# The last image's depthwise stage laid out over four engines by a list scheduler inside the kernel

## The chip, the cores and the metric

The kernel runs on one NeuronCore of a Trainium2 chip. The metric is device time in microseconds, the median of three runs. Five instruction streams work side by side[...]: TensorE (PE in the profile, its weight loads PEld), VectorE (DVE), ScalarE (ACT), GpSimd (POOL) and SyncE (SP), which here issues transfers.

## The reference, cut to what matters

Four residual layers run over four images of 256 channels and 64x64 pixels, all in float32. The change touches layer 2, whose weights are made from the image itself:

```python
def _L2_conv_ref(x, Wd1, bd1, Wd2, bd2, Wp1, bp1, Wp2, bp2, bias):
    dk = _gen_kernel(x, Wd1, bd1, Wd2, bd2).reshape(B, C, K, K)   # 3x3 taps for each image and channel
    pk = _gen_kernel(x, Wp1, bp1, Wp2, bp2).reshape(B, O, C)      # 256x256 matrix for each image
    dw = lax.conv_general_dilated(xr, kr, (STRIDE, STRIDE), [(PAD, PAD), (PAD, PAD)],
                                  feature_group_count=B * C)      # 3x3 depthwise, K = 3
    out = jnp.einsum('bchw,boc->bohw', dw, pk) + bias[None, :, None, None]
    return out
...
    x = x + _L2_conv_ref(_gn(x), ...)   # layer 2
    x = x + _L3_conv_ref(_gn(x), ...)   # layer 3: needs the group statistics of all of layer 2
```

`_gen_kernel` takes the mean over all pixels of a small hidden layer and multiplies it out, so no tap is known before the whole normalised image is.

## The kernel before

Channels are two halves `h` of 128 partitions. Pixels are four parts of 1024 (16 rows) or eight blocks of 512 (8 rows), one block to a PSUM bank. There are eight banks, handed out by `bank`[...]. `xp` holds the normalised image with a row of zeros above and below; `big` holds the residual, which for the last image lies in `tpg[:, 0:2]`.

Instructions are recorded by Python generators, and the order of recording is the order on each engine (`tc.manual_schedule`). For images 0 to 2 the layers of one image are woven into the attention of the next. The last image has nothing left to be woven into, so from about 2,800 us on its layers run alone, and the engines have to be filled by hand. One filler exists: layer 3 of image 2 is held back as 16 pieces (`held`). `w.fill(n)` issues the two matmuls of n pieces; `w.settle()` issues ScalarE's addition of the bias (L1819) and the store (L1820) for what was filled. A second filler is `warm(n)` (L355), 2n small matmuls on constants whose result nobody reads.

The last image's layer 2 is `generated` with `diag` set. Its steps:

- Group statistics (`group_finish`), then `hidden` (PE L1526, ACT L1529), whose sums over the pixels give `pooled`; a matmul spreads it over the partitions (L1550), and four small VectorE instructions make `dk`, the 2 x 9 taps of each partition.
- `shared_out` computes the depthwise outputs `dw`. Part i is (c, h): parts 0, 2, 4, 6 are half 0, parts 1, 3, 5, 7 half 1. `centre` (ACT L1572) writes the middle tap and `taps` (DVE, all through the helper `stt`, L140) adds the other eight, `dw = xp * dk + dw`, in SBUF. Parts 3 and 5, and seven taps of part 1, are done by TensorE instead: `taps_by_products` multiplies `xp` with a diagonal matrix of each tap (ACT L1674 makes the nine, PE L1631 multiplies) and ScalarE copies the bank out (L1634).
- `mix_kernel` makes `pk` by eight VectorE instructions from the four slices `wp2`, loaded at L1517.
- For each block of 512 pixels and each half of the outputs two matmuls with `pk` (L1580, and L1723 for the last part), then VectorE adds the result to the residual and sums it (L1592), and ScalarE squares and sums that (L1597).
- The sums and sums of squares of all 16 such pieces are needed (L385) before `mixed`, the last image's layer 3, can begin.

The order between these is written by hand in `shared_out`, for instance

```python
            dw[2] = centre(2)
            diagonal(27)
            go(0, 8)
            w.settle()
            mix_kernel(slices, range(0, R // 2))
            go(2, 3)
```

where `go(i, n)` takes n taps of part i on VectorE and `diagonal(n)` n products on TensorE. GpSimd does nothing in this stage.

## Time and profile before

| what | us |
|---|---|
| median of 3 runs (lowest, highest) | 2986.73 (2986.69, 2986.93) |
| the profiled execution's own time | 2988.41 |
| its span, from first to last instruction | 2986.7 |
| busy in the span: TensorE, VectorE, ScalarE, GpSimd | 2934.1, 1798.8, 1328.7, 136.8 |
| the last image's `dk` ready | 2862.28 |
| last residual sum of layer 2 ends (VectorE) | 2937.0 |
| last square ends, statistics begin | 2938.69 |
| first matmul of the last image's layer 3 | 2949.36 |

The span is 1.7 us shorter than that execution's time, and the execution 1.7 us longer than the median. Starts and durations below are microseconds from the span's start. A row of the timeline is one instruction or a merged run of like ones: start, time, engine, source line, operation, output<-inputs, shapes, count. [...]each matmul of the program is two records.

### The profile page before, as it was taken

To read this page: it belongs to the slowest core of one execution; us is meant where nothing else is said; L and a number is where in the kernel's file an instruction comes from. 1 tells how busy PE (TensorE), PEld (TensorE's weight loads), DVE (VectorE), ACT (ScalarE), POOL (GpSimd) and SP (SyncE) were. 2 spreads that over 40 slices of the span, in tenths; PEclk is the share of its full clock that TensorE was granted. 3 is DMA by queue.
4 is the path that set the end of the run, shared out by engine and by line. 5 is a ranking of instruction groups with operands and counts; after the bars stand their busy time and mean duration, and the time that the engine had idled before them with its cause. 6 is when DMAs were issued, how large, how long until landed. Compare 5 with 4: busy or idle time off the path is not lost.

```text
span 2986.7 us, 31274 instructions
## 1 busy us (share of the span) xinstructions
PE 2934.1 (98%) x11678; PEld 1785.7 (60%) x11678; DVE 1798.8 (60%) x2785; ACT 1328.7 (44%) x2674; POOL 136.8 (5%) x185
## 2 busy tenths in 40 slices
PE   7999999999999999999999999999999999999998
PEld 3454555566566666777576666777647544456744
DVE  8737667751645854675455583667154568854584
ACT  2234333445656344225665543323656554433732
POOL 0000000001011000000011000000100100000100
PEclk9999999999999999999999999999999999999999
DMA  6245544224323012111620303111440223443021
GB/s 227 74 85 122 67 67 75 39 32 99 113 39 43 22 78 75 57 57 33 188 37 11 50 8 124 57 54 49 92 92 11 25 42 46 32 95 90 24 69 68
DMA packets 371295, 199.38 MB, mean 67 GB/s; under 512 B 305664, under 2 KB 315648, under 8 KB 367616
## 3 DMA queue, kind: packets, MB, share of 16 engines
q1 hardware_dynamic: 71328, 175.81, 17.5%
q10 hardware_dynamic: 295200, 4.72, 7.9%
q0 software_dynamic: 4608, 16.78, 3.7%
q8 instruction: 94, 1.54, 0.2%
q14 instruction: 65, 0.53, 0.1%
HBM read 131.18 MB, written 82.87 MB: 72 GB/s over the span
## 4 chain that ended last, share of the span: by engine, by line
PE 76%; issue 19%; DVE 2%; ACT 2%; POOL 0%; DMA 0%; ACTq 0%; DVEq 0%; POOLq 0%
PE pf L1013 24%; PE py L1129 16%; PE py L1126 8%; PE ps_tp L951 4%; PE ps_ex L1811 4%; PE ps_qk L1316 3%; PE ps_pw L1580 3%; PE ps_conv L663 2%; PE ps_ctx L1343 2%; PE ps_o L1414 2%; PE ps_g L956 2%; PE ps_dw L1631 1%; PE ps_wy L1066 1%; ACT big L760 1%; PE ps_xt L1296 1%
## 5 line engine op out<-in xcount | busy, mean ns | idle before, releaser
L1014 ACT ACTIVATE pr<-pf 128x512 f32<-128x512 f32 x1024 | 602.7, 596 | 911.3 <-PE pf L1013 889.9
L1013 PE MATMUL pf<-tpg 128*128 128x512 f32 x2048 | 966.4, 594 | 0.0
L1013 PEld LDWEIGHTS pf<-tpg 128*128 128x128 f32 x2048 | 374.1, 190 | 358.4 <-issue 336.4
L1129 PE MATMUL py<-pr,tpg 128*128 128x512 f32 x1152 | 541.6, 592 | 0.9 <-ACT pr L1014 0.9
L1126 PEld LDWEIGHTS py<-tpg,pr 128*128 128x128 f32 x3584 | 434.9, 192 | 108.0 <-issue 100.7
L1126 PE MATMUL py<-tpg,pr 128*128 128x129 f32 x3584 | 436.3, 275 | 2.4 <-ACT pr L1014 2.4
L1129 PEld LDWEIGHTS py<-pr,tpg 128*128 128x128 f32 x1152 | 218.6, 190 | 277.4 <-issue 268.3
L137 DVE TENSOR_TENSOR tot<-tot,pr 128x1024 f32<-128x1024 f32 x252 | 307.6, 1221 | 98.5 <-ACT pr L1014 98.0
L140 DVE SCALAR_TENSOR_TENSOR dw<-xp,dk,dw 128x1008 f32<-128x1008 f32 x208 | 263.3, 1270 | 8.0 <-ACT dw L1572 2.4
L663 PE MATMUL ps_conv<-v,u 128*128 128x256 f32 x864 | 195.6, 379 | 2.3 <-DVE v L137 2.3
L663 PEld LDWEIGHTS ps_conv<-v,u 128*128 128x128 f32 x864 | 161.5, 190 | 31.3 <-issue 8.4
L951 PE MATMUL ps_tp<-big,wtpg_s 128*128 128x512 f32 x256 | 117.1, 596 | 4.7 <-ACT big L760 4.0
L232 POOL TENSOR_TENSOR rstd<-rstd,half 128x2 f32<-128x2 f32 x24 | 17.5, 731 | 2173.4 <-DVE rstd L427 2063.0
L137 DVE TENSOR_TENSOR tpg<-ps_g,bg_s 128x512 f32<-128x512 f32 x32 | 22.1, 692 | 155.2 <-PE ps_g L956 155.2
L1316 PE MATMUL ps_qk<-wqkv_s,xg 128*128 128x256 f32 x496 | 113.6, 379 | 0.0
L140 DVE SCALAR_TENSOR_TENSOR sums<-ps_conv,sums 128x512 f32<-128x512 f32 x72 | 49.8, 691 | 103.9 <-PE ps_conv L663 97.5
L1316 PEld LDWEIGHTS ps_qk<-wqkv_s,xg 128*128 128x128 f32 x496 | 93.8, 190 | 20.4 <-issue 8.4
L1580 PE MATMUL ps_pw<-dw,pk 128*128 128x512 f32 x216 | 97.4, 592 | 0.0
L951 PEld LDWEIGHTS ps_tp<-big,wtpg_s 128*128 128x128 f32 x256 | 45.8, 190 | 54.7 <-issue 41.8
L952 ACT ACTIVATE tpg<-ps_tp,btp_s 128x512 f32<-128x512 f32 x64 | 44.0, 687 | 70.4 <-PE ps_tp L951 70.4
L1079 DVE COPY total<-py 128x2 f32<-128x2 f32 x28 | 4.5, 159 | 115.6 <-PE py L1126 115.6
L1819 ACT ACTIVATE res<-ps_ex,b 128x512 f32<-128x512 f32 x56 | 38.1, 688 | 76.5 <-PE ps_ex L1811 74.6
(400 smaller groups left out, 3280.3 us busy)
## 6 DMA issues: line engine op xcount, KB each, us to landing
u<-filters SPq DMA_DIRECT2D x72, 256.0 KB, 2.6
xp<-in_x_dram SPq DMA_DIRECT2D x16, 1024.0 KB, 8.4
xs_d<-big POOLq DMA_DIRECT2D x32, 512.0 KB, 6.3
wy_d<-wt SPq DMA_DIRECT2D x32, 512.0 KB, 2.8
wy<-wy_d SPq DMA_DIRECT2D x32, 512.0 KB, 4.7
out_dram<-res SPq DMA_DIRECT2D x64, 256.0 KB, 2.0
xs_d<-in_x_dram SPq DMA_DIRECT2D x24, 512.0 KB, 6.6
xs<-xs_d SPq DMA_DIRECT2D x24, 512.0 KB, 5.2
```

Source lines behind the costliest of these rows:

```text
L137: nc.vector.tensor_tensor(o, a, b, op)
L140: nc.vector.scalar_tensor_tensor(o, a, s, b, op0, op1)
L663: nc.tensor.matmul(ps[:, bass.ts(oh, IY * IX)], u[i][:, h, bass.ts(oh, P)], v[:, i, bass.ts(h, IY * IX)], start=(h == 0), stop=(h == NH - 1))
L951: nc.tensor.matmul(ps, wtpg_s[:, h, k, :], big[:, h, cols], start=(h == 0), stop=(h == NH - 1))
L956: nc.tensor.matmul(ps[:, j, :], big[:, h, bass.ts(4 * c + j, P)], wtpg_s[:, h, 2, :], start=(h == 0), stop=(h == NH - 1))
L1013: nc.tensor.matmul(pf, phi[:, bass.ts(2 * m + s, P)], theta[:, bass.ts(q, 512)], start=True, stop=True)
L1014: nc.scalar.activation(pr[:, bass.ts(s, 512)], pf, AF.Exp)
L1126: nc.tensor.matmul(py[t // 2][:, t % 2, :], probs[i][:, s * 512 + t * P:s * 512 + (t + 1) * P], g[:, 2 * m + s, :], start=(begin and t % 2 ...
L1129: nc.tensor.matmul(py, g[:, 2 * m + s, 0:P], probs[i][:, bass.ts(s, 512)], start=begin, stop=end)
L1316: nc.tensor.matmul(ps[:, 0:2 * HID], xg[:, h, bass.ts(j, P)], wqkv_s[:, h, 0:2 * HID], start=(h == 0), stop=(h == NH - 1))
L1580: nc.tensor.matmul(ps, pk[:, h * NH * P + oh * P:h * NH * P + (oh + 1) * P], dw[h][:, bass.ts(s, 512)], start=(h == 0), stop=(h == NH - 1))
L1811: nc.tensor.matmul(ps, wm[h][:, bass.ts(oh, P)], big[:, h, bass.ts(c, 512)], start=(h == 0), stop=(h == NH - 1))
```

## The change

The hand-written order of `shared_out` goes, with `taps_by_products`. In its place `halves_of_three` splits the work into 16 half parts `(k, h)`, a block of 512 pixels of one half of the channels, and gives each to one engine: five to GpSimd (`ON_POOL`), three wholly to TensorE and two in part (`ON_TENSOR` counts the products), the rest to VectorE. VectorE's taps now accumulate in a PSUM bank; only the last one writes SBUF. GpSimd's part is the addition alone: ScalarE first writes the scaled tap into one of five SBUF tiles of 512 (the free end of `tpg[:, 2]`), and GpSimd adds it. `mix_kernel` becomes `mixing`, which accumulates in a bank too. All of it, the squares and the additions left over from `fill` included, is a list of jobs with an engine, a duration, predecessors and a rank; `emit_by_start` places them by these durations, and the order of the result is the order of recording. The durations serve for nothing else.

Around it five calls change: `fill(2)` becomes `fill(3)` at the end of linear attention, `warm(3)` becomes `fill(1)` after the statistics of layer 2, `settle` and `fill(1)` between the `hidden` blocks go, `fill(3)` after the pooling matmul becomes `fill(1)`, and 16 small matmuls of `warm` ahead of layer 3's statistics become `fill(1)`. The loads of `wp2` are issued behind that of `pk`, before the normalisation.

```diff
-            w.fill(2)
+            w.fill(3)
...
+    ENDING = [t for t in TAPS if t[1] != 1] + [(0, 1), (2, 1)]
+    ALL = [(1, 1)] + ENDING
+    ON_POOL = ((0, 0), (1, 1), (2, 0), (4, 1), (6, 0))
+    ON_TENSOR = {(0, 1): 1, (3, 1): 7, (5, 1): 9, (6, 1): 9, (7, 1): 9}
+    HALVES = [(0, 0), (3, 0), (1, 0), (3, 1), (7, 0), (5, 0), (0, 1), (6, 0), (6, 1), (2, 1), (2, 0), (4, 0), (1, 1), (5, 1),
+              (7, 1), (4, 1)]
+    TAP_TILES = 5
...
+    def emit_by_start(jobs, free, banks):
...
+                    if on == engine and all(a in ends for a in after) and len(spare) >= takes:
+                        at = [ends[a][1] + (0.2 if ends[a][0] != on else 0.0) for a in after]
+                        ready.append((max([free[on]] + at + sorted(spare)[:takes]), rank, j))
...
         if diag is not None:
-            warm(3)
+            w.fill(1)
...
+        if diag is not None:
+            slices = [load_wp2(j) for j in range(R // 2)]
...
-            if c == NC3:
+            if c == NC3 and diag is None:
                 w.settle()
                 w.fill(1)
...
-        w.fill(3)
+        w.fill(3 if diag is None else 1)
...
+            def middle(k, h, bank_of):
+                if bank_of:
+                    banks[k, h] = bank("ps_acc")
+                nc.scalar.activation(pixels(banks[k, h] if bank_of else half_tile(k, h)), xin[:, h, bass.ts(k, RB), :],
+                                     AF.Copy, scale=weight(h, (1, 1)))
...
+                    to = half_tile(k, h) if t == ENDING[-1] else acc
+                    stt(pixels(to)[:, :, x0:x1], src, weight(h, t), pixels(acc)[:, :, x0:x1], ALU.mult, ALU.add)
...
+                nc.scalar.activation(pixels(scaled_taps[n])[:, :, x0:x1], src, AF.Copy, scale=weight(h, t))
...
+                nc.gpsimd.tensor_tensor(acc, acc, pixels(scaled_taps[n])[:, :, x0:x1], ALU.add)
...
+            for n, f in enumerate(w.unsettled):
+                job(("late", n), E.Activation, 0.66, [], 4 + 1.5 * n, f, 0, ["late"])
...
+            emit_by_start(jobs, {E.PE: 0.5, E.Activation: 0.1, E.DVE: 0.0, E.Pool: 0.0}, 8 - late)
...
-        mv, gm, rstd = yield from group_finish(st, avg8, 1e-5, sh, (), (8, 1) if alone else (0, 0))
+        if alone:
+            w.fill(1)
+        mv, gm, rstd = yield from group_finish(st, avg8, 1e-5, sh, (), (0, 1) if alone else (0, 0))
```

On each engine the recorded order after `dk` begins as follows. VectorE: eight of `mixing`, four taps of (0,1), eight of (3,0), eight of (1,0). ScalarE: middle and taps of (0,0) with the nine diagonals between them. TensorE: one product of (0,1), nine of (6,1), seven of (3,1). GpSimd: the eight additions of (0,0), (6,0), (2,0), (1,1) and (4,1) in turn. The last on TensorE, VectorE and ScalarE are the matmuls, sums and squares of block 4.

More of the change, by code (lines that the diff above doesn't have):

```diff
@@ L1486, in conv_preact_fast @@
     TAPS = [(i, j) for i in range(3) for j in range(3) if (i, j) != (1, 1)]
+    ENDING = [t for t in TAPS if t[1] != 1] + [(0, 1), (2, 1)]
[6 more added lines that the diff above has]
+    def emit_by_start(jobs, free, banks):
+        ends, spare, left = {}, [0.0] * banks, list(jobs)
+        while left:
+            best = None
+            for engine in free:
+                ready = []
+                for j in left:
+                    name, on, us, after, rank, emit, takes, frees = j
+                    if on == engine and all(a in ends for a in after) and len(spare) >= takes:
+                        at = [ends[a][1] + (0.2 if ends[a][0] != on else 0.0) for a in after]
+                        ready.append((max([free[on]] + at + sorted(spare)[:takes]), rank, j))
+                if ready:
+                    first = min(r[0] for r in ready)
+                    pick = min((r for r in ready if r[0] <= first + 0.05), key=lambda r: r[1])
+                    if best is None or pick[0] < best[0]:
+                        best = pick
+            start, _, (name, on, us, after, rank, emit, takes, frees) = best
+            left.remove(best[2])
+            emit()
+            free[on] = start + us
+            ends[name] = on, free[on]
+            spare = sorted(spare)[takes:] + [free[on] + 0.1] * len(frees)
     def generated(w, b, big, k4, st, sh, diag):
+        if diag is not None:
+            diag, diag_all = diag
         if diag is None:
@@ L1518, in load_wp2 @@
             return t
+        if diag is not None:
+            slices = [load_wp2(j) for j in range(R // 2)]
         def hidden(g):
@@ L1565, in generated @@
         rows = CH // HW
+        if diag is not None:
+            diag_rest = diag_all[:, 9 * P:]
         PARTS = [(c, h) for c in range(N // CH) for h in range(NH)]
@@ L1616, in taps @@
                 yield 0.66
-        def taps_by_products(parts):
-            for i, some in parts:
-                c, h = PARTS[i]
-                dw[i] = k4("dw")
-                for s in range(2):
-                    ps = bank("ps_dw")
-                    dst = ps.rearrange("p (y x) -> p y x", x=HW)
-                    for n, (ty, tx) in enumerate([(1, 1)] + some):
-                        dx = tx - 1
-                        x0, x1 = max(0, -dx), min(HW, HW - dx)
-                        y0 = (2 * c + s) * RB + ty
-                        nc.tensor.matmul(dst[:, :, x0:x1], diag[:, 3 * ty + tx, :], xp[:, h, y0:y0 + RB, x0 + dx:x1 + dx],
-                                         start=(n == 0), stop=(n == len(some)))
-                        if n == len(some):
-                            nc.scalar.copy(dw[i][:, bass.ts(s, 512)], ps)
-                        yield
         def mix_kernel(slices, js):
@@ L1665, in in_order, with halves_of_three @@
             yield from w.pending()
-        def shared_out():
-            slices = [load_wp2(j) for j in range(R // 2)]
+        def halves_of_three():
             yield from w.pending()
-            products = taps_by_products([(1, TAPS[:6]), (3, TAPS), (5, TAPS)])
-            dw[0] = centre(0)
-            for k in range(9):
-                nc.scalar.activation(diag[:, k, :], ident, AF.Copy, scale=dk[:, 9 + k:10 + k])
-            on_vector = {i: taps(i) for i in (0, 2, 4, 6)}
-            on_vector[1] = taps(1, TAPS[6:])
-            def go(i, n):
-                for _ in range(n):
-                    next(on_vector[i])
-            def diagonal(n):
-                for _ in range(n):
-                    next(products)
-            def point(c):
-                d = [dw[2 * c + h] for h in range(NH)]
-                return [(2 * c + s, pointwise_products(s, d)) for s in range(2)]
-            dw[2] = centre(2)
-            diagonal(27)
-            go(0, 8)
-            w.settle()
-            mix_kernel(slices, range(0, R // 2))
-            go(2, 3)
-            mix_kernel(slices, range(R // 2, R))
-            go(1, 2)
-            go(2, 5)
-            dw[4] = centre(4)
-            res = point(0)
-            diagonal(5)
-            pointwise_added(*res[0])
-            go(4, 1)
-            pointwise_added(*res[1])
-            go(4, 7)
-            dw[6], dw[7] = centre(6), centre(7)
-            res = point(1)
-            diagonal(18)
-            go(6, 1)
-            pointwise_added(*res[0])
-            go(6, 2)
-            pointwise_added(*res[1])
-            go(6, 5)
-            ends = [taps(7, TAPS, slice(s * RB, (s + 1) * RB)) for s in range(2)]
-            for _ in ends[0]:
-                pass
-            res = point(2)
-            banks = [[bank("ps_pw") for _ in range(NH)] for _ in range(2)]
-            def half(s, h):
-                for oh in range(NH):
-                    nc.tensor.matmul(banks[s][oh], pk[:, h * NH * P + oh * P:h * NH * P + (oh + 1) * P],
-                                     dw[6 + h][:, bass.ts(s, 512)], start=(h == 0), stop=(h == NH - 1))
-            half(0, 0)
-            half(0, 1)
-            half(1, 0)
-            pointwise_added(*res[0])
-            for _ in ends[1]:
-                pass
-            half(1, 1)
-            pointwise_added(*res[1])
-            for s in range(2):
-                pointwise_added(6 + s, banks[s])
@@ new lines, in halves_of_three, with job, pixels, half_tile @@
+            scaled_taps = [diag_rest[:, bass.ts(n, 512)] for n in range(TAP_TILES)]
+            tiles, banks, wide = {}, {}, 63 / 64
+            jobs, chain = [], []
+            def job(name, engine, us, after, rank, emit, takes=0, frees=()):
+                jobs.append((name, engine, us, after, rank, emit, takes, frees))
+            def pixels(t):
+                return t.rearrange("p (y x) -> p y x", x=HW)
+            def half_tile(k, h):
+                if (k // 2, h) not in tiles:
+                    tiles[k // 2, h] = k4("dw")
+                return tiles[k // 2, h][:, bass.ts(k % 2, 512)]
@@ new lines, in shifted, with weight @@
+            def shifted(k, h, ty, dx):
+                x0, x1 = max(0, -dx), min(HW, HW - dx)
+                return x0, x1, xp[:, h, k * RB + ty:(k + 1) * RB + ty, x0 + dx:x1 + dx]
+            def weight(h, t):
+                return dk[:, h * 9 + 3 * t[0] + t[1]:h * 9 + 3 * t[0] + t[1] + 1]
+            def middle(k, h, bank_of):
[3 more added lines that the diff above has]
+                                     AF.Copy, scale=weight(h, (1, 1)))
@@ new lines, in on_vector, with scaled_tap @@
+            def on_vector(k, h, some):
+                acc = banks[k, h]
+                for t in some:
+                    x0, x1, src = shifted(k, h, t[0], t[1] - 1)
+                    to = half_tile(k, h) if t == ENDING[-1] else acc
+                    stt(pixels(to)[:, :, x0:x1], src, weight(h, t), pixels(acc)[:, :, x0:x1], ALU.mult, ALU.add)
+                if to is not acc:
+                    del banks[k, h]
+            def scaled_tap(k, h, t, n):
+                x0, x1, src = shifted(k, h, t[0], t[1] - 1)
+                nc.scalar.activation(pixels(scaled_taps[n])[:, :, x0:x1], src, AF.Copy, scale=weight(h, t))
@@ new lines, in on_pool, with on_tensor @@
+            def on_pool(k, h, t, n):
+                x0, x1, _ = shifted(k, h, t[0], t[1] - 1)
+                acc = pixels(half_tile(k, h))[:, :, x0:x1]
+                nc.gpsimd.tensor_tensor(acc, acc, pixels(scaled_taps[n])[:, :, x0:x1], ALU.add)
+            def on_tensor(k, h, some, last):
+                if some[0] == ALL[0]:
+                    banks[k, h] = bank("ps_dw")
+                for t in some:
+                    x0, x1, src = shifted(k, h, t[0], t[1] - 1)
+                    nc.tensor.matmul(pixels(banks[k, h])[:, :, x0:x1], diag[:, 3 * t[0] + t[1], :], src,
+                                     start=(t == ALL[0]), stop=(t == last))
@@ new lines, in taken, with diagonals, mixing @@
+            def taken(k, h):
+                nc.scalar.copy(half_tile(k, h), banks.pop((k, h)))
+            def diagonals(some):
+                for ty, tx in some:
+                    nc.scalar.activation(diag[:, 3 * ty + tx, :], ident, AF.Copy, scale=weight(1, (ty, tx)))
+            def mixing(j):
+                first, last = j == 0, j == R - 1
+                if first:
+                    banks["pk"] = bank("ps_pk")
+                acc = banks["pk"]
+                stt(pk if last else acc, slices[j // 2][:, j % 2, :], pb[:, R + j:R + j + 1], pk if first else acc,
+                    ALU.mult, ALU.add)
+                if last:
+                    del banks["pk"]
@@ new lines, in point, with added @@
+            def point(k, oh):
+                ps = banks[k, "out", oh] = bank("ps_pw")
+                for h in range(NH):
+                    nc.tensor.matmul(ps, pk[:, h * NH * P + oh * P:h * NH * P + (oh + 1) * P],
+                                     tiles[k // 2, h][:, bass.ts(k % 2, 512)], start=(h == 0), stop=(h == NH - 1))
+            def added(k, oh):
+                cols = bass.ts(k, 512)
+                nc.vector.scalar_tensor_tensor(big[:, oh, cols], banks.pop((k, "out", oh)), 1.0, big[:, oh, cols], ALU.mult,
+                                               ALU.add, accum_out=sums[:, 0, oh, k:k + 1])
@@ new lines, in square @@
+            def square(k, oh):
+                nc.scalar.activation(junk(), big[:, oh, bass.ts(k, 512)], AF.Square, bias=pivot[:, oh:oh + 1],
+                                     accum_out=sums[:, 1, oh, k:k + 1])
+            for j in range(R):
+                job(("mix", j), E.DVE, 0.65, [("mix", j - 1)] if j else [], -5, lambda j=j: mixing(j),
+                    j == 0, ["mix"] if j == R - 1 else [])
+            for n in range(3):
+                job(("diag", n), E.Activation, 0.97, [], -0.85 + 0.25 * n, lambda n=n: diagonals(ALL[3 * n:3 * n + 3]))
@@ new lines, in halves_of_three @@
+            late = len(w.unsettled)
+            for n, f in enumerate(w.unsettled):
+                job(("late", n), E.Activation, 0.66, [], 4 + 1.5 * n, f, 0, ["late"])
+            w.unsettled = []
+            done = {}
+            for rank, (k, h) in enumerate(HALVES):
+                x = (k, h)
+                products = ON_TENSOR.get(x, 0)
+                if x not in ON_POOL and products < 9:
+                    if products:
+                        last = ("t", x, 0)
+                        job(last, E.PE, 0.857 * products, [("diag", i) for i in range(-(-products // 3))], rank - 2,
+                            lambda x=x, n=products: on_tensor(*x, ALL[:n], ALL[n - 1]), 1)
+                    else:
+                        last = ("mid", x)
+                        job(last, E.Activation, 0.66, [], rank - 1.5, lambda x=x: middle(*x, True), 1)
+                    rest = ALL[max(1, products):]
+                    while rest:
+                        name, some, rest = ("v", x, len(rest)), rest[:2], rest[2:]
+                        job(name, E.DVE, 0.74 * len(some), [last], rank, lambda x=x, some=some: on_vector(*x, some), 0,
+                            [] if rest else ["v"])
+                        last = name
+                    done[x] = last
+                elif x not in ON_POOL:
+                    for i in range(3):
+                        job(("t", x, i), E.PE, 2.57, [("diag", i)] + [("t", x, i - 1)] * (i > 0), rank,
+                            lambda x=x, i=i: on_tensor(*x, ALL[3 * i:3 * i + 3], ALL[-1]), i == 0)
+                    job(("taken", x), E.Activation, 0.6, [("t", x, 2)], rank - 1.5, lambda x=x: taken(*x), 0, ["t"])
+                    done[x] = ("taken", x)
+                else:
+                    job(("qm", x), E.Activation, 0.66, [], rank - 0.9, lambda x=x: middle(*x, False))
+                    for i, t in enumerate(ENDING):
+                        n = len(chain)
+                        job(("qt", x, i), E.Activation, 0.64, [chain[n - TAP_TILES]] if n >= TAP_TILES else [], rank - 0.9 + 0.1 * i,
+                            lambda x=x, t=t, n=n: scaled_tap(*x, t, n % TAP_TILES))
+                        job(("q", x, i), E.Pool, 1.32, [("qt", x, i), ("qm", x)] + chain[-1:], rank,
+                            lambda x=x, t=t, n=n: on_pool(*x, t, n % TAP_TILES))
+                        chain.append(("q", x, i))
+                    done[x] = ("q", x, 7)
@@ new lines, in halves_of_three @@
+            for k in range(N // 512):
+                rank = max(HALVES.index((k, h)) for h in range(NH))
+                for oh in range(NH):
+                    job(("out", k, oh), E.PE, 1.72, [done[k, h] for h in range(NH)] + [("mix", R - 1)] + [("out", k, 0)] * oh, rank - 0.5,
+                        lambda k=k, oh=oh: point(k, oh), 1)
+                    job(("sum", k, oh), E.DVE, 0.65, [("out", k, oh)], rank - 1.2, lambda k=k, oh=oh: added(k, oh), 0, ["out"])
+                    job(("sq", k, oh), E.Activation, 0.85, [("sum", k, oh)], rank + 1.5, lambda k=k, oh=oh: square(k, oh))
@@ L1739, in generated @@
         else:
-            yield from shared_out()
+            yield from halves_of_three()
         sh2 = sp.tile([P, NH], F32, name="sh2")
@@ L1905, in conv_preact_fast @@
         spare = [t.rearrange("p h y x -> p h (y x)")[:, h, 0:CH] for t in (ra, rt) for h in range(NH)]
-        diag = tpg[:, NH, 0:9 * P].rearrange("p (k q) -> p k q", k=9)
+        diag = tpg[:, NH, 0:9 * P].rearrange("p (k q) -> p k q", k=9), tpg[:, NH, :]
         attention = attend(B - 1)
```

## The prediction

> **What bounds the kernel now.** The page says TensorE is busy for 98% of the span; that is the mean over a run of which this change touches some 90 us. So I read the stage alone: the busy time by stretches for the last image's depthwise stage, from taps ready (2862.2) to last square (2938.7).

> ```profile
> core 0: us, PE busy (x) PEld busy (x) DVE busy (x) ACT busy (x) POOL busy (x), PEclk, DMA share, GB/s
> 2862.20:2938.70 76.50, 76.50 (x197) 35.39 (x196) 70.45 (x93) 26.80 (x57) 0.00 (x0) 1.00 0.19 62
> ```

> Two engines are full, ScalarE idles for two thirds, GpSimd does nothing. Next the timeline of VectorE there, then what starts layer 3:

> ```profile
> 2863.49 10.43 DVE L140 SCALAR_TENSOR_TENSOR ra<-xp,dk,ra 128x1008 f32<-128x1008 f32 x8 [1.22 <-ACT ra L1572]
> 2873.84 3.11 DVE L140 SCALAR_TENSOR_TENSOR pk<-wp,pb,pk 128x512 f32<-128x512 f32 x4
> ...
> 2926.70 6.21 DVE L140 SCALAR_TENSOR_TENSOR rt<-xp,dk,rt 128x504 f32<-128x504 f32 x8
> ...
> 2936.38 0.69 DVE L1592 SCALAR_TENSOR_TENSOR tpg<-ps_pw,tpg 128x512 f32<-128x512 f32 x1 [0.16 <-PE ps_pw L1723]
> 2938.69 0.19 DVE L385 TENSOR_REDUCE both_m<-sums 128x4 f32<-128x32 f32 x1 [1.54 <-ACT junk L1597]
> ```

> VectorE runs its taps without a gap (idle in brackets is only ever about 1 us), and the statistics wait for the last square, which trails the last sum. TensorE's products occupy it as long, one record each 0.43 us:

> ```profile
> 2866.25 14.18 PE L1631 MATMUL ps_dw<-xp,tpg 128*128 128x512 f32 x33
> ```

> After 2938.69 comes a serial tail to the end of the span, 48.0 us, in which the change alters only fillers. So the time is decided by when the last square ends.

> **The removed and added work, engine by engine.** Durations are start-to-start distances where rows follow one another, since a row's own length overlaps the next.

> *VectorE.* A 512-pixel tap in a dependent run is 6.21 / 8 = 0.776 us, a step of `pk` 3.11 / 4 = 0.778, a sum 0.61 (rows at 2893.22 and 2893.83), a 1024-pixel tap 10.43 / 8 = 1.30. Before: 34 x 1.30 + 16 x 0.776 + 8 x 0.778 + 16 x 0.61 = 44.2 + 12.4 + 6.2 + 9.8 = 72.6 of the 73.5 us from 2863.49 to 2937.0. After: GpSimd has 5 half parts, TensorE 3; six have 8 taps left on VectorE, (0,1) 8, (3,1) 2, together 58: 58 x 0.776 + 6.2 + 9.8 = **61.0**. It also starts at once, with `mixing` at 2862.28, where it waited 1.22 us for `centre`.

> The new taps write into PSUM, and no row of VectorE does that. Reading it costs nothing visible: the addition of a transposed bank takes 0.741 (L140 from `ps_zt`), the tap from SBUF 0.743. I take 0.776, and for the range 0.70 (0.61, the distance between independent sums, plus some of the dependence) to 0.85 (a tenth dearer).

> *TensorE.* 35 products instead of 50, 32 matmuls with `pk` as before, each two records of 0.427: 67 x 0.855 = 57.3 us, from 70.1. Two pieces of filler fewer behind the pooling matmul: another 3.4 gone.

> *ScalarE.* No row of it is a scaled copy of 512 from SBUF. Nine of 128x128 take 2.72 (0.302 each), two of 1024 stand 1.04 apart; the straight line gives 0.615 for 512. 40 scaled taps, 11 middle taps, 5 left-over additions: 56 x 0.615 = 34.4; diagonals 2.7, three copies out 1.7, 16 squares 0.85 apart 13.6. Sum 52.4: it has room for what it is given.

> *GpSimd.* 40 additions of 504 or 512 elements in one chain. The trace has none; its nearest rows are powers:

> ```profile
> L232 POOL TENSOR_TENSOR rinv<-rinv,half 128x4 f32<-128x4 f32 x32 | 32.7, 1021 | 223.1 <-DVE rinv L1300 217.7 <-DMA wy<-wy_d 5.4
> L232 POOL TENSOR_TENSOR rstd<-rstd,half 128x2 f32<-128x2 f32 x24 | 17.5, 731 | 2173.4 <-DVE rstd L427 2063.0 <-DVE nb L137 110.4
> ```

> Two more elements cost 0.29, so 0.44 us is fixed; the slope is a power's and says nothing of an addition. [...] I take [...]**1.33**. [...]at 1.33 GpSimd is far slower than VectorE, but it is idle, and 40 x 1.33 = 53 us lie beside VectorE's 61.

> **The four queues laid end to end.** I put every instruction in its recorded order, each starting when its engine is free and its inputs are done, plus 0.2 us behind TensorE (the copy at 2922.65 follows its product's stream by that) and 0.1 behind the others (a 1.14 us row of ScalarE against its distance of 1.04). Counted from `dk`:

> - VectorE runs without a gap to 56.7. The taps of (0,1) and (3,1) need TensorE's products only long after these are done (at 21.7 against 17.1).
> - TensorE starts at 2.3, behind the first diagonals. Its queue is in order: the matmuls of block 3 stand behind the products of (5,1) and wait for VectorE until 23.4, and the second group of (7,1) must pass before later blocks. From 27 on it is almost never idle; the last eight pairs of matmuls, 1.71 each, run from 48.8 to **62.5**.
> - GpSimd ends at 1.4 + 40 x 1.33 = 55, before block 4 is wanted (59).
> - The last sum waits for the last pair: 62.5 + 0.2 + 0.61, then 0.1 and a square of 0.85: **64.2**.

> Before, the same point is 2938.69 - 2862.28 = 76.4. **The stage gains 12.2 us.** VectorE's work and TensorE's tail tie as the bound.

> **The edits around it.**
> - `fill(3)` for `fill(2)`: 1.7 us of matmuls in TensorE's idle 2.0 before 2849.07. Cost 0, with 0.3 to spare.
> - `fill(1)` for `warm(3)`: the warm matmuls end at 2852.6 and hold the next (L1509), whose input is ready at 2852.04. Four records of 0.43 end at 2852.2. Gain 0.3.
> - `fill(1)` and `settle` gone before the pooling: its matmul no longer queues behind four records. Gain 0.2. The two additions on ScalarE lay in its wait for `dk`: 0.
> - The loads of `wp2` (512 KB each, landing 6.9 us after issue) move to SP behind the load of `pk` at 2836.9, 25 us before `mixing` needs the first. Behind them on SP stand stores not wanted before the additions of this stage. Cost 0; if a load were late, the wait would now be first on VectorE and in full.
> - `fill(1)` for 16 small matmuls before the last statistics: beside the last sums and squares, 0.

> *The clock* is the fourth effect of the fillers. In the stretches around 2851 the granted clock falls:

> ```profile
> 2848.00:2850.00 2.00, 0.94 (x6) 1.00 0.00 0
> 2850.00:2852.00 2.00, 1.71 (x12) 0.84 0.00 0
> 2852.00:2854.00 2.00, 2.00 (x22) 0.50 0.01 4
> 2854.00:2856.00 2.00, 2.00 (x15) 0.81 0.00 0
> ```

> (stretch, length, TensorE busy, granted clock, DMA). Half speed lasts from 2851.4 to 2854.8, and the hidden matmuls (L1526) begin in it: their first two steps are 0.85 apart, later ones 0.43, so 0.86 us is lost on the path to `dk`. [...] By the rows it falls after 3.4 us with only some 1.3 us of streaming matmuls in them (twelve warm records of 0.11), while 2940.1 to 2943.5, with about fifteen, 1.7 us, kept full speed. The change adds 0.65 us to the first of these windows, 1.95 in all. I go by the rows: no fall, **gain 0.86**.

> By the same measure two new thin places are doubtful: about half of the 3.4 us around TensorE's 2 us gap at the start of the stage is streamed, and as much during the last statistics, where 1.3 us of warm matmuls are missing. A fall costs about 1 us at the first (TensorE loses 1.7 and has 0.75 to spare) and up to 1.4 at the second (the last fill before layer 3). I count neither and keep both for the range.

> **Sum.** -12.2 - 0.3 - 0.2 - 0.86 = -13.6. The profiled execution goes from 2988.4 (span 2986.7) to 2974.8 (2973.1). The median of the runs shown is 1.7 lower than that execution; there I forecast **2973.2 us**. No change is what lies within 0.2%, 6 us.

> **Rivals.**
> - *GpSimd takes VectorE's place as the bound.* With p for an addition the end is 1.4 + 40p + 5.3 (two pairs of matmuls, sum, square). It decides from p = 1.44; at 1.55 the stage takes 68.7, so 2977.7, at 1.70 it is 2983.7. For it: the fixed 0.44 and two semaphore waits in every link of the chain.[...]
> - *VectorE in PSUM is dearer.* 0.85 instead of 0.776 adds 58 x 0.074 = 4.3: 2977.5; 0.90 gives 2980.4. At 0.70 TensorE's tail holds 61.3: 2970.3. For it: no row; against: reads show nothing.
> - *Slower than before: GpSimd holds block 4.* The same chain, at its end: (4,1) is last in GpSimd's queue, and the last matmuls, sums and squares stand behind it. The gain of 1.4 before the stage included, it loses from 1.4 + 40p + 5.3 = 77.8, p = 1.78; at 2.0 it takes 86.7 and gives 2995.7. [...]
> - *It does not do what it says.* The recorded order is fixed, so the work moves as planned; only the durations can betray it.

> **Chances.** Forecast, with clock falls or without, 2969.8 to 2977: 0.70. GpSimd at 1.44 to 1.78: 0.14, of which 0.10 is still over 0.2% faster. VectorE dearer: 0.09, 0.08 of it faster. GpSimd above 1.78: 0.07, 0.06 slower, 0.01 no change. Faster 0.88, same 0.06, slower 0.06. The range 2969.8 to 2980 leaves out the dear ends of the rivals and a little below, some 0.15.

> **What would show it.** In the changed trace: additions on GpSimd 1.33 apart and ending by 57 after `dk`; taps 0.78 apart with `ps_acc` as output; no VectorE gap over 1.2 us before the last sums; last square 64 after `dk`; `dk` near 2860.9; clock 1.00 at 2852. GpSimd's distances over 1.44, or VectorE's growing only while GpSimd works, would make the prediction wrong.

## The result and the profile after

The changed kernel takes **2971.4 us**, the median of six executions (2970.5 to 2974.2), where the kernel before takes 2986.7: a ratio of 0.9951, 95% interval 0.9941 to 0.9961. Forecast was 2973.2. In a second set of five executions its median was 2973.43 (0.9956, 0.9943 to 0.9970); why the two sets differ is part of what follows. The profiled execution took 2974.19 us with a span of 2972.4, against 2974.8 and 2973.1 forecast.

The two spans are laid side by side at five points that each has:

| stretch | before | after | difference | forecast |
|---|---|---|---|---|
| start to the mean's matmul of layer 2 (L409) | 2849.07 | 2847.31 | -1.76 | 0 |
| from there to `dk` ready | 13.21 | 11.85 | -1.36 | -1.36 |
| `dk` to the last square | 76.41 | 63.12 | -13.29 | -12.2 |
| last square to the first matmul of the last layer 3 | 10.67 | 13.49 | +2.82 | 0 |
| from there to the end | 37.34 | 36.63 | -0.71 | 0 |
| span | 2986.7 | 2972.4 | -14.3 | -13.6 |

The sum is right to 0.7 us, in part by luck: the stage gained 1.1 us more than forecast, and the three rows that were forecast as nothing (-1.76, +2.82, -0.71) nearly cancel. First the stage itself, as busy time (stretch, its length, then for each engine busy time and instructions, granted clock, DMA share and rate):

```profile
core 0: us, PE busy (x) PEld busy (x) DVE busy (x) ACT busy (x) POOL busy (x), PEclk, DMA share, GB/s
2859.16:2922.28 63.12, 61.14 (x140) 25.72 (x138) 58.20 (x100) 51.78 (x100) 50.46 (x40) 1.00 0.11 38
```

Before, two engines were full and GpSimd empty; now four work for 50 us or more of 63. VectorE's and GpSimd's rows on the timeline of the changed kernel:

```profile
2868.28 5.45 DVE L140 SCALAR_TENSOR_TENSOR ps_acc<-xp,dk,ps_acc 128x504 f32<-128x504 f32 x7
2874.43 5.45 DVE L140 SCALAR_TENSOR_TENSOR ps_acc<-xp,dk,ps_acc 128x504 f32<-128x504 f32 x7
...
2918.92 0.69 DVE L1771 SCALAR_TENSOR_TENSOR tpg<-ps_pw,tpg 128x512 f32<-128x512 f32 x1 [1.02 <-PE ps_pw L1766]
2920.64 0.69 DVE L1771 SCALAR_TENSOR_TENSOR tpg<-ps_pw,tpg 128x512 f32<-128x512 f32 x1 [1.02 <-PE ps_pw L1766]
2922.28 0.18 DVE L385 TENSOR_REDUCE both_m<-sums 128x4 f32<-128x32 f32 x1 [0.87 <-ACT junk L1775]
```

```profile
2893.20 10.66 POOL L1736 TENSOR_TENSOR dw<-dw,tpg 128x504 f32<-128x504 f32 x8
2903.82 10.66 POOL L1736 TENSOR_TENSOR rt<-rt,tpg 128x504 f32<-128x504 f32 x8
```

A tap that accumulates in PSUM is 5.45 / 7 = 0.78 us, as it was in SBUF. Eight additions start 10.62 apart, 1.33 each, and GpSimd ends at 2914.48, 55.3 after `dk`. Which engine carries the end is read from the chain of waits, followed back from the last instruction (start, length, piece):

```profile
2885.12 0.61 DVE tpg L1771 x2
2885.86 3.93 PE ps_pw L1766 x8
2889.79 7.65 PE ps_dw L1743 x18
2897.44 6.87 PE ps_pw L1766 x16
2904.30 2.56 PE ps_dw L1743 x6
2906.86 13.75 PE ps_pw L1766 x32
2920.64 0.70 DVE tpg L1771 x2
```

Before 2885.12 the chain runs on VectorE alone (`mixing`, then taps without a break); from 2885.86 to 2920.6 it runs on TensorE alone. The bound is handed over 26 us into the stage.

The row that grew, +2.82, is seen in the granted clock (last number but two of each line):

```profile
2924.00:2926.00 2.00, 1.71 (x10) 1.52 (x10) 0.94 (x7) 0.00 (x0) 0.39 (x1) 0.72 0.04 8
2926.00:2928.00 2.00, 2.00 (x11) 1.76 (x11) 0.32 (x3) 0.00 (x0) 0.32 (x1) 0.50 0.00 0
2928.00:2930.00 2.00, 2.00 (x7) 1.62 (x7) 0.43 (x2) 0.33 (x3) 0.00 (x0) 0.50 0.00 0
2930.00:2932.00 2.00, 2.00 (x4) 0.76 (x3) 1.80 (x7) 0.60 (x2) 0.00 (x0) 0.57 0.26 101
```

From 2924.9 to 2931.7 TensorE runs at half speed, in the middle of the serial path to layer 3. The row that shrank ahead of the change, -1.76, is for the most part (1.68) a halved clock of the kernel before at 2810.4 to 2813.8, in code that the change does not touch; the same 24 records of linear attention are on TensorE's timeline of before, and then of after:

```profile
2809.95 7.13 PE L1414 MATMUL ps_o<-w,tpg 128*128 128x256 f32 x24 [0.52 <-DVE w L140]
```

```profile
2809.67 5.45 PE L1414 MATMUL ps_o<-w,tpg 128*128 128x256 f32 x24 [0.52 <-DVE w L140]
```

The last row, -0.71, arises behind the last matmul, in the end of the output (7.8 us before, 7.1 after); its cause stays open.

### The profile page after: what moved, and what is told of

The parts are those of the page before. It is cut to its first block, busy times and chain, and to the rows that moved or that the text cites. A ratio compares the mean times of both kernels' runs of the same rounds, so it can differ in the third digit from the quotient of the medians.

```text
span 2972.4 us, 31260 instructions
## 1 busy us (share of the span) xinstructions
PE 2918.3 (98%) x11604; PEld 1776.5 (60%) x11604; DVE 1785.9 (60%) x2793; ACT 1352.4 (45%) x2717; POOL 187.1 (6%) x225
## 4 chain that ended last, share of the span: by engine, by line
PE 78%; issue 16%; DVE 3%; ACT 2%; DMA 1%; POOL 0%; SPq 0%; DVEq 0%; ACTq 0%; POOLq 0%
PE pf L1013 24%; PE py L1129 16%; PE py L1126 8%; PE ps_tp L951 4%; PE ps_qk L1316 3%; PE ps_ex L1907 3%; PE ps_pw L1620 3%; PE ps_conv L663 2%; PE ps_ctx L1343 2%; PE ps_o L1414 2%; PE ps_g L956 2%; PE ps_row L617 1%; PE ps_conv L578 1%; PE ps_wy L1066 1%; ACT big L760 1%
## 5 line engine op out<-in xcount | busy, mean ns | idle before, releaser
L137 DVE TENSOR_TENSOR tot<-tot,pr 128x1024 f32<-128x1024 f32 x252 | 307.5, 1220 | 98.6 <-ACT pr L1014 98.1
L140 DVE SCALAR_TENSOR_TENSOR dw<-xp,dk,dw 128x1008 f32<-128x1008 f32 x192 | 242.9, 1270 | 7.6 <-ACT dw L1612 2.4
L232 POOL TENSOR_TENSOR rstd<-rstd,half 128x2 f32<-128x2 f32 x24 | 17.5, 730 | 2093.8 <-DVE rstd L427 1983.4
L137 DVE TENSOR_TENSOR tpg<-ps_g,bg_s 128x512 f32<-128x512 f32 x32 | 22.1, 691 | 155.6 <-PE ps_g L956 155.6
L140 DVE SCALAR_TENSOR_TENSOR sums<-ps_conv,sums 128x512 f32<-128x512 f32 x72 | 49.7, 691 | 104.0 <-PE ps_conv L663 97.6
L1620 PE MATMUL ps_pw<-dw,pk 128*128 128x512 f32 x192 | 86.3, 592 | 0.0
```

Of the source, the lines that this page charges most:

```text
L137: nc.vector.tensor_tensor(o, a, b, op)
L140: nc.vector.scalar_tensor_tensor(o, a, s, b, op0, op1)
L1620: nc.tensor.matmul(ps, pk[:, h * NH * P + oh * P:h * NH * P + (oh + 1) * P], dw[h][:, bass.ts(s, 512)], start=(h == 0), stop=(h == NH - 1))
```

## The experiments

Below, "stage" is from `dk` to the last square and "tail" from there to the first matmul of the last layer 3 (63.12 and 13.49 in the changed kernel, 76.41 and 10.67 before), each from the profiled execution of the run.

### Is the longer tail the fillers' doing?

`warm_back` puts 16 small matmuls, 32 records, back behind the `fill(1)`; `after_again` is the changed kernel itself.

```diff
-        mv, gm, rstd = yield from group_finish(st, avg8, 1e-5, sh, (), (0, 1) if alone else (0, 0))
+        mv, gm, rstd = yield from group_finish(st, avg8, 1e-5, sh, (), (8, 1) if alone else (0, 0))
```

> The changed kernel with the 16 small matmuls put back ahead of the last statistics, beside the fill(1) that replaced them. Theory (clock): the tail from the last square to the end of the span, 48.0 us before the change and 50.1 after it, is longer because TensorE streams too little in the 3.4 us around the last statistics and its clock is halved; with the small matmuls back the granted clock stays 1.00 there, the tail is 48.0 again and the profiled execution some 2 us shorter than the changed kernel's 2972.4 of span; the median falls to about 2970. Rival (chance): whether the clock falls there depends only on where its window happens to lie, so the tail stays at 50.1 in some executions and the scatter of 3.6 us between executions remains. Rival (cost): the matmuls stand in the way of the statistics' own and the tail grows by up to 0.5.

> The changed kernel itself once more, beside warm_back on the same chip. Theory (clock): executions scatter between about 2970.5 and 2974.2, as in its first six runs, and a second profile shows its halved stretches of the clock at other places than the first, or the one at the last statistics again. Rival (work): the scatter comes from the stage itself, whose length then differs from 63.1 us by more than 1 us in the second profile.

`warm_back`: median 2973.29 (five executions between 2972.94 and 2973.40), clock 1.00 throughout the tail, stage 63.12, tail 12.76. The expected fall to 2970 did not come, and TensorE's timeline tells why:

```profile
2922.13 3.73 PE L355 MATMUL ps_warm<-ident,ones 128*128 128x128 f32 x32
2925.70 0.28 PE L409 MATMUL pm<-mv,avg 128*128 128x2 f32 x2
```

The small matmuls now stand behind a fill that ends at 2922.1 and run for 3.6 us more, so the mean's matmul starts 3.45 us after the statistics begin (2922.25) instead of 1.30. The clock is saved and 2.1 us are lost in the queue; the rival on cost was right in kind, but it allowed 0.5 us.

`after_again`: median 2973.43 (2970.84 to 2973.73). Its profiled execution is the one of 2970.84: stage 63.12 again, clock 1.00 in the tail, tail 10.67; the clock was at half from 2838.6 to 2842.0 instead. The eleven executions of this kernel lie in two groups, five at 2970.5 to 2971.4 and six at 2972.8 to 2974.2. The one profile taken in the upper group has the halved clock in the tail, the one taken in the lower has not. So the stage is steady in both profiles, and between them the same program loses 2.8 us or not according to where the clock falls. For the other nine executions that is inferred; of the second set the mean granted clock is on record, 0.999 for the fastest and 0.997 to 0.998 for the rest.

`warm_few` takes 4 small matmuls, 8 records: `(2, 1)` in the line above.

> The changed kernel with 8 warm records (4 small matmuls) instead of 32 behind the fill(1) ahead of the last statistics. In warm_back the 32 kept the clock at 1.00 but ran to 3.45 us after the last square and held the mean's matmul 2.1 us, so that both effects cancelled. Theory (clock and queue): 8 records take 0.9 us and end before the mean's input is ready (1.3 us after the last square), so the matmul is not held, and the 3.4 us window there streams about 2 us instead of 1.2, so the clock does not fall: from the last square to the first matmul of layer 3 10.67 us in every execution, none at 2973 or more from this cause, median 2970.8. Rival (not enough): the clock still falls in about half of the executions, which then lie 2.8 us higher, median about 2972 to 2973. Rival (queue): the 8 hold the matmul too, +0.5.

Median 2970.72, four executions at 2970.53 to 2971.17 and one at 2972.99. TensorE's timeline:

```profile
2922.32 1.05 PE L355 MATMUL ps_warm<-ident,ones 128*128 128x128 f32 x8
2923.75 0.38 PE L409 MATMUL pm<-mv,avg 128*128 128x2 f32 x2 [0.38 <-DVE mv L137]
```

The eight end before the mean's input is ready (the wait of 0.38 shows it), the matmul starts 1.31 after the statistics begin, the clock stays at 1.00 and the tail is 10.72. This is what the theory said, though one profile and four executions of five are a weak proof against a fall that comes about half of the time. The fifth execution had a lower mean clock (0.998, the four 0.999); where it fell is not known. In `tensor_minus_one` below, with the same filler, the profile again shows no fall in the tail.

### Stage and fillers apart

`stage_alone` has the new stage with the five filler calls of before; `calls_alone` the old stage with the new calls (contrary to its expectation, the loads of `wp2` stay where they were).

```diff
-            w.fill(3)
+            w.fill(2)
...
-            w.fill(1)
+            warm(3)
...
-            if c == NC3 and diag is None:
+            if c == NC3:
...
-        w.fill(3 if diag is None else 1)
+        w.fill(3)
...
-        if alone:
-            w.fill(1)
-        mv, gm, rstd = yield from group_finish(st, avg8, 1e-5, sh, (), (0, 1) if alone else (0, 0))
+        mv, gm, rstd = yield from group_finish(st, avg8, 1e-5, sh, (), (8, 1) if alone else (0, 0))
```

> The four-engine stage with the fillers of before (five calls put back). Theory (sum): without the fillers' part the gain ahead of the stage, 1.36 us, is gone, with a halved clock at 2851 where the window lies as before; inside the stage TensorE starts behind the three pieces after the pooling, about 4.0 us behind dk instead of 1.7, and as its tail ties with VectorE the stage grows from 63.1 to about 65; tail 48.0. Sum about -11.4, median near 2975. Rival (VectorE alone bounds): the stage stays at 63.1 though TensorE starts later, median near 2973.4. Rival (fillers carry the stage): the stage is over 68.

> The stage of before with the five changed filler calls and the earlier loads of wp2. Theory (sum): 1.36 us less from the mean matmul to dk (0.3 + 0.2 + 0.86) and no halved clock at 2851; the stage itself stays at 76.4, since VectorE bounds it and TensorE's earlier start changes nothing; then, if the clock falls at the last statistics, 2.1 us more in the tail. Median 2985.3, or 2987.4 with that fall. Rival (TensorE bounds too): the two pieces less behind the pooling shorten the stage by up to 3.4, median near 2982.

`stage_alone`: median 2975.21 (ratio 0.9963, 0.9949 to 0.9976), stage 64.43. In this run an execution's time is 3.1 to 3.8 us longer than its span, in all others 1.5 to 2.2; why is not known. So the spans are the better measure: median 2971.4, against 2971.6 for the changed kernel and 2984.6 for the kernel before in the same set. That the time came out near the forecast of 2975 is therefore partly luck. TensorE's timeline behind the pooling:

```profile
2860.79 5.40 PE L1905 MATMUL ps_ex<-big,wmh 128*128 128x512 f32 x12
2866.03 14.17 PE L1743 MATMUL ps_dw<-xp,tpg 128*128 128x512 f32 x33
```

`dk` was ready at 2862.05, so TensorE starts its products 3.98 us behind it instead of 1.71, and 1.31 of these 2.27 us arrive at the end of the stage: TensorE's load binds there, with about 1 us of slack. From the mean's matmul to `dk` it takes 14.69, with the clock at half from 2848.3 to 2855.1 around `warm(3)`, against 11.85.

`calls_alone`: 13 executions from 2983.6 to 2991.2, median 2985.47, ratio 1.0003 (0.9994 to 1.0011), no change. Its profiled execution (span 2982.5, nowhere at half speed in the region) shows 11.85 to `dk`, as summed, and a stage of 75.24. VectorE's waits for block matmuls (L1580) went from 1.4 to 0.3 us, as its rows show, first before, then here:

```profile
2896.25 0.69 DVE L1592 SCALAR_TENSOR_TENSOR tpg<-ps_pw,tpg 128x512 f32<-128x512 f32 x1 [0.55 <-PE ps_pw L1580]
2926.08 0.69 DVE L1592 SCALAR_TENSOR_TENSOR tpg<-ps_pw,tpg 128x512 f32<-128x512 f32 x1 [0.82 <-PE ps_pw L1580]
```

```profile
2922.36 0.69 DVE L1592 SCALAR_TENSOR_TENSOR tpg<-ps_pw,tpg 128x512 f32<-128x512 f32 x1 [0.30 <-PE ps_pw L1580]
```

So TensorE bounded the old stage for about 1.1 us. The rival had that at up to 3.4. Both gains are there in the profile, and the scatter of 7.6 us covers them. The scatter goes with the clock: the six executions up to 2984.7 have a mean granted clock of 0.998 or 0.999, the seven from 2985.5 on 0.995 to 0.997. So the gain of the change is the stage's, about 13 us of span with the old calls as with the new. What the new calls save ahead of the stage and in it shows in the profiles, and in no median of the spans (2971.4 against 2971.6 with the new stage); that the clock at the last statistics takes it back is likely and not shown.

### What GpSimd may cost

A further addition of 128 elements, on an own tile, stands behind every fourth, every second and each of GpSimd's 40 additions, and twice behind each.

```diff
+            own = diag_rest[:, 5 * 512:5 * 512 + 128]
+            nc.gpsimd.memset(own, 0.0)
...
                 nc.gpsimd.tensor_tensor(acc, acc, pixels(scaled_taps[n])[:, :, x0:x1], ALU.add)
+                if t in ENDING[3::4]:
+                    nc.gpsimd.tensor_tensor(own, own, own, ALU.add)
```

> The changed kernel with a further GpSimd addition of 128 elements on an own tile behind every fourth of its 40 additions (nothing of the result changes). Theory (the prediction's formula): with p the mean distance of the 40 additions the stage takes the larger of 63.1 and 1.4 + 40p + 5.3; if the further one takes 0.5 to 0.7, p is 1.46 to 1.51 and the stage 65 to 67. Rival (slack): GpSimd ends before its results are wanted by more than the formula says, and the stage stays at 63.1. Rival (cascade): waits for GpSimd pile up at several blocks, and the stage is over 68.

> The changed kernel with a further GpSimd addition of 128 elements on an own tile behind every second of its 40 additions (nothing of the result changes). In pool_plus_quarter one such addition took 0.35 us, p was 1.41 and the stage stayed at 63.1. Theory (the prediction's formula 1.4 + 40p + 5.3, which decides from p = 1.44, or 1.41 against the measured 63.1): p = 1.33 + 0.35 / 2 = 1.51, stage 67.0, span about 2973. Rival (slack): GpSimd's results are wanted later than the formula says, stage 63 to 65. Rival (cascade): over 69.

> As pool_plus_half, with the further addition behind each of the 40. Theory: p = 1.68, stage 73.9, span about 2980, still faster than before. Rival (cascade): waits for GpSimd add up at several blocks, TensorE's and VectorE's work is pushed behind its end, and the stage is over 77, as long as before.

> As pool_plus_half, with two further additions behind each of the 40. Theory: p = 2.03, stage 87.9, the kernel near 2996 and slower than before, as the prediction's third rival puts it (2995.7 at p = 2.0); the change breaks even at p = 1.78. Rival (cascade): the kernel is over 3000.

The runs of this table, and `vector_sbuf` below, are single executions but for the changed kernel.

| run | p (first start to last end, by 40) | last addition ends after `dk` | stage | stage less that | time |
|---|---|---|---|---|---|
| changed kernel | 1.35 | 55.3 | 63.12 | 7.8 | 2971.4 |
| `pool_plus_quarter` | 1.40 | 57.4 | 63.12 | 5.7 | 2970.85 |
| `pool_plus_half` | 1.46 | 59.8 | 64.36 | 4.6 | 2972.25 |
| `pool_plus_all` | 1.57 | 64.3 | 68.90 | 4.6 | 2979.28 |
| `pool_plus_two` | 2.03 | 82.8 | 89.91 | 7.2 | 2998.25 |

The form of the rule holds; two terms were off. The further addition made p rise by less than expected, as these rows of `pool_plus_all` show (GpSimd, then TensorE):

```profile
2919.88 1.39 POOL L1738 TENSOR_TENSOR rt<-rt,tpg 128x512 f32<-128x512 f32 x1
2921.10 0.52 POOL L1740 TENSOR_TENSOR tpg<-tpg 128x128 f32<-128x128 f32 x1
2921.46 1.39 POOL L1738 TENSOR_TENSOR rt<-rt,tpg 128x512 f32<-128x512 f32 x1
```

```profile
2917.78 3.60 PE L1770 MATMUL ps_pw<-dw,pk 128*128 128x512 f32 x8
2922.90 1.13 PE L1770 MATMUL ps_pw<-rt,pk 128*128 128x512 f32 x2 [1.53 <-POOL rt L1738]
```

The pair of an addition and a further one is 1.58 long (2919.88 to 2921.46): the further one starts 1.22 behind its addition, where the next addition of the chain comes only after 1.33, so it costs 0.25 net. And behind the last addition (end 2922.85, TensorE resumes at 2922.90) only three of block 4's four matmuls are left: the first, whose input is VectorE's, had run ahead. What is left is 4.6 us, not 5.3. The 4.6 is read from `pool_plus_half` and `pool_plus_all`, and is the same in both. With it the stage is 1.44 + 40p + 4.6; 63.1 is reached at p = 1.43, and the change breaks even at (77.8 - 6.0) / 40 = 1.79, a value between two runs that no run tests. `pool_plus_two` lies 2.6 us above the rule and is slower than the kernel before, as the third rival would have been: TensorE, waiting for GpSimd, was at half speed from 2937.0 to 2947.2 and ran the last six records of block 4 so, 6 x 0.43 = 2.6 us longer. The time of `pool_plus_all` has a fall of the clock in its tail too (13.60), as the changed kernel's profile has.

### Is PSUM only a place, or a condition?

In the changed kernel the taps that accumulate in a bank ran at 0.78 us beside GpSimd's additions at 1.33. In `vector_sbuf` the six half parts that are all VectorE's accumulate in SBUF, so that 48 of 58 taps have two SBUF inputs. The recorded order is the same.

```diff
-                acc = banks[k, h]
+                acc = banks[k, h] if (k, h) in ON_TENSOR else half_tile(k, h)
...
-                    to = half_tile(k, h) if t == ENDING[-1] else acc
+                    to = half_tile(k, h) if t == ENDING[-1] or (k, h) not in ON_TENSOR else acc
```

> The changed kernel with VectorE's accumulation in SBUF for the six half parts without products (48 of 58 taps, both inputs in SBUF) beside GpSimd's additions. Theory (lock[...]): 48 x 0.776 = 37 us of VectorE and 40 x 1.33 = 53 of GpSimd cannot overlap, the stage is over 85 us, the kernel over 2993, taps and additions far from 0.78 and 1.33 while both work. Rival (no lock between these forms): taps 0.78, additions 1.33, stage 63 to 64, kernel about 2972. Between the two, partial blocking would show as additions of 1.4 to 2.

2998.55 us, stage 88.8. VectorE's timeline, and GpSimd's:

```profile
2866.99 3.09 DVE L140 SCALAR_TENSOR_TENSOR ps_dw<-xp,dk,ps_dw 128x504 f32<-128x504 f32 x4
2869.99 12.70 DVE L140 SCALAR_TENSOR_TENSOR dw<-xp,dk,dw 128x504 f32<-128x504 f32 x8
2882.61 13.33 DVE L140 SCALAR_TENSOR_TENSOR ra<-xp,dk,ra 128x504 f32<-128x504 f32 x8
2897.31 3.08 DVE L140 SCALAR_TENSOR_TENSOR ra<-xp,dk,ra 128x504 f32<-128x504 f32 x4
```

```profile
2863.86 23.27 POOL L1736 TENSOR_TENSOR ra<-ra,tpg 128x504 f32<-128x504 f32 x15 [0.29 <-ACT tpg L1731]
2902.59 1.28 POOL L1736 TENSOR_TENSOR dw<-dw,tpg 128x512 f32<-128x512 f32 x1 [5.54 <-ACT tpg L1731]
2907.09 13.00 POOL L1736 TENSOR_TENSOR rt<-rt,tpg 128x504 f32<-128x504 f32 x8
```

With the accumulator in PSUM four taps take 3.09, 0.77 each; in SBUF, beside GpSimd, eight take 12.70, 1.59 each, and the additions grow from 1.33 to 1.6. One tap and one addition together take 1.6, more than either alone (0.78, 1.33) and less than both in turn (2.1). So the two hold each other up, but not in full: some 0.5 us of a pair overlaps (0.78 + 1.33 - 1.6), an estimate from these three numbers. That SBUF is not dear by itself, the same run shows: GpSimd is idle for 5.5 us ahead of 2902.59, and there four taps with two SBUF inputs take 3.08, 0.77 each. No wait on a semaphore joins the two engines in these rows: from 2860 to 2950 VectorE waits 2.1 us for ScalarE and 0.5 for TensorE, and for GpSimd not at all. Part of the 88.8 is a consequence: the clock is at half from 2885.6 to 2902.6 and from 2916.3 to 2923.1, when TensorE waits for both.

### A load less on TensorE

`tensor_minus_one` is `warm_few` with the single product of half part (0,1) given back to ScalarE as a middle tap: `ON_TENSOR = {(3, 1): 7, ...}`. VectorE's taps stay 58; the list scheduler finds another order.

> As warm_few, and the one product of half part (0,1) on TensorE becomes a middle tap on ScalarE; VectorE's taps stay 58. The list scheduler makes another order of it. Theory (TensorE's tail binds the stage, VectorE only ties): TensorE has 0.86 us less, the stage falls from 63.1 to about 62.1, median about 1.0 below warm_few. Rival (VectorE's 61 us bind): no change of the stage, 63.1. Rival (order): the other order makes new waits and the stage is longer than 63.1.

Median **2969.77** (ratio to the kernel before 0.9945, 0.9932 to 0.9959), four executions at 2969.25 to 2969.84, stage 62.24 (63.12 in `warm_few`), that is 0.88 less for a product of 0.86. With 2985 to 2986.5 for the kernel before in the same set, this is the best version, 0.95 below `warm_few`, 1.6 and 3.7 below the two medians of the changed kernel; the intervals of the ratios overlap, and the two sets of four lie apart. The fifth execution, 2971.99, is the profiled one, and its clock was at half from 2810.3 to 2813.7, as that of the kernel before: it reaches the mean's matmul at 2849.01, where `warm_few` is at 2847.47. The order differs too, so the size of the gain fits TensorE's load and does not prove it alone.

## Why the prediction was right, point by point

- *VectorE 61.0.* Right to 1.0 us: from its first `mixing` to the end of its last sum are 62.2 us with 2.2 of waits, so 60.0 of work; taps 0.78 (0.776 taken), sums 0.61. PSUM cost nothing, and the rival of a dearer VectorE did not occur.
- *GpSimd at 1.33, ending at 55.* Right, 1.33 and 55.3. The value was the author's estimate, of which the trace of before shows no more than the 0.44 in its powers, so that it fits to the hundredth is luck. At 1.55, which the prediction weighs as well, the measured terms give about 68 (1.44 + 62 + 4.6) where it had 68.7.
- *TensorE's tail.* Right in place, 1.1 us too late: its last eight pairs run 47.7 to 61.4 behind `dk` (48.8 to 62.5 forecast). 0.6 of that is its start, 1.7 behind `dk` and not 2.3. "Tie" was too weak a word: the chain, `stage_alone` and `tensor_minus_one` all say that TensorE carries the end, with VectorE waiting 2.2 us for it. A second term was hidden in the base: `calls_alone` shows that TensorE bounded 1.1 us of the stage before as well.
- *The edits around it, -1.36.* Right in the profiled pair, with no fall of the clock at 2852 as the rows had argued. The parts are 0.20, 0.15 and, for the clock, 1.01, where 0.3, 0.2 and 0.86 were forecast, so the agreement to the hundredth is luck. With the calls of before, both profiles (before and `stage_alone`) have a fall there; whether each execution has it is not known, and `calls_alone` shows no gain at the median.
- *The clock at the last statistics.* The failed step: "up to 1.4" and not counted, it was 2.82 in the profiled execution, because two stretches of 3.4 us ran at half speed, not one, and every matmul on the serial path was in them, where the sum had only the last fill. It was named as the doubtful place, and by the executions' two groups it comes about half of the time.
- *Start of the stage.* No fall there in the profiles of the changed kernel: the gap on TensorE was 0.99, not 2.
- *The base.* The -1.76 ahead of the change (all but 0.1) and the +2.82 behind it are both the clock's. The prediction subtracted 1.7 for the profiled execution's distance to the median without knowing what it was. The fall at 2810 costs 1.7 us and may be it; whether the executions at the median lacked it is not shown.
- *Rival "GpSimd holds block 4".* Its threshold stands (1.79 by the measured terms, 1.78 forecast; p = 1.57 was faster, p = 2.03 slower than before), and in the changed kernel p is 1.35. What keeps it there is that the taps accumulate in PSUM: with two SBUF inputs for 48 of them the kernel is at 2998.55, within 3 us of what the rival gave for p = 2.0. That closeness is chance: its p is 1.87, for which 1.44 + 40p + 4.6 gives 81 and not 88.8, since VectorE is slowed too and the clock falls.

## What to carry to other kernels

When work goes to GpSimd, look first at where VectorE's operands lie: one accumulator in PSUM decided between 13 to 15 us gained and 12 us lost here, at the same instruction counts and the same order. After balancing engines, follow the chain in order of time and not only the sums of busy time: it shows who binds last, and that engine is the one to relieve next. Fillers for the clock have a place in a queue: count when they end against when the next real matmul's input is ready, and too many cost nearly as much (2.1 us) as too few (2.8).

## What was not expected of the hardware

- The clock's fall is a matter of position. In programs that are alike up to 2838, stretches at half speed lay at 2810 (before, `tensor_minus_one`, `vector_sbuf`), at 2838 (`after_again`, `stage_alone`, `pool_plus_two`) or at neither place. In the changed kernel the step ahead of 2924.9 holds about 1.1 us of streaming by the count above (0.65 of the fill, the rest small matmuls), and the clock fell. In `after_again` the two steps there, laid from its own fall at 2838.6, hold 1.6 and 1.5, and the clock stayed. This fall needed no step without work: the longest gap on TensorE ahead of 2924.9 was 1.27 us.
- An addition of 504 elements on GpSimd in a dependent chain is 1.33 from start to start; in `pool_plus_all` an independent one of 128 elements followed after 1.22 and took 0.36 more.
- A late engine cost TensorE its clock as well: in `pool_plus_two` TensorE waited 7.57 us for GpSimd and then ran at half speed, 2.6 us on top of the wait.
